# An exchange through DRAM: all four of its writes issued by SyncE instead of two by SyncE and two by ScalarE

## The chip, the cores and the metric

The kernel runs on one core of a Trainium2 chip. The metric is the device time of one execution in microseconds (us), median over runs. The engines are named as the profile names them: PE (TensorE matmul), PEld (its weight loads), DVE (VectorE), ACT (ScalarE), POOL (GpSimd) and SP (SyncE). A "q" behind a name (SPq, ACTq) is the engine's sequencer, which issues DMAs.

## The reference

For x of 8 sequences x 128 tokens x 512 features, all in float32, the reference computes two residual blocks:

```python
x = x + ffn0(lora_matmul(x, weight[ids]))      # 8 adapters; top-2 of 8 low-rank experts
x = x + ffn1(attention(x))                     # below; then top-16 of 64 rank-8 experts

q = rope(rmsnorm(x @ Wq)); k = rope(rmsnorm(x @ Wk)); v = x @ Wv   # 32 q heads, 8 kv heads, D = 128
k_all = concat(k_cache[pages], k); v_all = concat(v_cache[pages], v)   # 512 cached + 128 new keys
p = softmax(mask(q @ k_all.T * D**-0.5)); y = (p @ v_all) @ Wo
```

Four query heads share one kv head. The cached keys and values lie in pages of 32 tokens, found through a table of page numbers; keys beyond a sequence's length are masked.

## The kernel before, in words

The first block runs in a stage of its own (about the first 120 us). The attention then runs as 64 *units*. A unit is one sequence and one kv head with its 4 query heads; two units in a row are the two kv heads of one *step* and share the step's cached keys and values. The order of all instructions is written out by hand, with no scheduler: each engine executes its own in program order, and semaphores between engines follow from the data.

`iteration(u)` is the pipeline. In it PE computes the scores of unit u, head by head (`scores`, L793 and L796), then the output projection of unit u-3 (`output`, L895), a slice of the q, k, v projection of a later unit (`project`, L259), and last the product of probabilities and values of unit u-2 (`values`, L873). DVE adds the mask and scales (`mask_exp`, L806), ACT takes the exponential (L817), DVE the reciprocal of its sum (L822), POOL scales by it (L823).

The probabilities have to be turned (keys on the partitions) before PE can use them. PE doesn't do that. DVE transposes blocks of 32 x 32 within groups of 32 partitions (`blocks`, L828, and `blocks_qk`, L779, for the rotated q and k of unit u+2) into the tile pb. What is left is to move whole blocks between the four groups of 32 partitions, and that is done by DMA through DRAM:

- `exchange_out(u)` (L840) writes pb to a DRAM tile px with four DMAs, one for each group of 32 partitions (i = 0 to 3). Each moves 32 x 4 rows of 3200 bytes (2560 where no later q and k ride along).
- `exchange_in(u)` (L850 and L853, both SP), one iteration later, reads qkb (q and k of unit u+2) and pT (the probabilities) back from px, block-transposed.

pb has one buffer, so L779 of the next unit can't write into it until all four writes have read it. px has three DRAM buffers, qkb one, pT two. From qkb ACT makes qkT, the queries and keys for the scores (`heads_qk`, L860), between the last exponential and the sums of squares of a later unit (`norms`, L308). POOL turns those into rs (L314), and DVE needs rs to rotate k (L340) right after the exchange. ACT also copies the attention output o to oT (`evict_o`, L884) at the head of the next iteration.

SP has, in program order, in each iteration: three pages of cached keys (`gather`, L193 to L194: for each page it loads a page number into a register, then issues a DMA of 32 KB), `exchange_in(u-1)`, the other pages (seven in even units, three in odd ones), in some iterations a load of ya (L143) and a store to yd (L919) of a partial sum, and at the end its part of `exchange_out(u)`. POOL issues the weights (L153, L177) and gathers the values vt (L204) from its own queue. ACT issues no DMA in the attention except its part of the exchange. In the DMA view queue q1 is SP's, q10 ACT's, q0 POOL's.

Of the kernel before, what the change touches and what calls it, by code (L numbers as in the profile page):

```python
# [33 lines left out]
QD = P // 32  # L34
# [23 lines left out]
def adaln_ffn_kernel(  # L58
# [25 lines left out]
    nc = tc.nc  # L84
# [667 lines left out]
    with ExitStack() as l1:  # L752
# [80 lines left out]
        def exchange_out(u):  # L833

            pb = pb_t.pop(u)
            m = dram_x.tile([QD, 32, QD, XW], F32, tag="px", name=f"px_{u}")
            w = XW if u + 2 in range(3, NU) else PW
            for i in range(QD):
                eng = nc.sync if i < QD // 2 else nc.scalar
                eng.dma_start(  # L840
                    out=m[:, :, i, :w].rearrange("k b f -> b k f"),
                    in_=pb[i * 32 : (i + 1) * 32, :, :w],
                )
            px_t[u] = m
# [114 lines left out]
        def iteration(u):  # L959
# [98 lines left out]
            if on(u):  # L1058
                blocks(u, REP - 2)
                blocks(u, REP - 1)  # L1060
                exchange_out(u)
# [176 lines left out]
```

## Time and profile before

| | before |
|---|---|
| median of 3 runs | 1248.08 us |
| lowest, highest | 1246.36, 1251.02 us |
| the profiled execution, its own time | 1243.45 us |
| its span (first to last instruction) | 1241.7 us |
| granted TensorE clock | 0.997 |
| mean DMA rate over the span | 241 GB/s |

The page describes the one profiled execution. Its span is 1.75 us shorter than its time. "Busy" is the time in which an engine executed instructions of the program. A timeline line gives the start, the length (of the merged run of instructions), the engine and line, what is written from what, how many instructions, and in brackets how long the engine had stood idle and what ended it. A line of the stages view gives, for a stretch of the span, each engine's busy time and number of instructions, the granted clock, the busy share of the 16 DMA engines and what they moved. The trace also holds a record of each DMA packet: its queue, size, start and length.

### The profile page before, as it was taken

To read this page: it belongs to the slowest core of one execution; us is meant where nothing else is said; L and a number is where in the kernel's file an instruction comes from. 1 tells how busy PE (TensorE), PEld (TensorE's weight loads), DVE (VectorE), ACT (ScalarE), POOL (GpSimd) and SP (SyncE) were. 2 spreads that over 40 slices of the span, in tenths; PEclk is the share of its full clock that TensorE was granted. 3 is DMA by queue.
4 is the path that set the end of the run, shared out by engine and by line. 5 is a ranking of instruction groups with operands and counts; after the bars stand their busy time and mean duration, and the time that the engine had idled before them with its cause. 6 is when DMAs were issued, how large, how long until landed. Compare 5 with 4: busy or idle time off the path is not lost.

```text
span 1241.7 us, 15991 instructions
## 1 busy us (share of the span) xinstructions
PE 1224.1 (99%) x3847; PEld 650.6 (52%) x3847; DVE 902.4 (73%) x2045; ACT 506.6 (41%) x1457; POOL 590.7 (48%) x687
## 2 busy tenths in 40 slices
PE   8999899999999999999999999999999999999998
PEld 7765455554555555555455555554555555555444
DVE  2546798889877777788877777788777777787522
ACT  1334444444444444444444444444444444443211
POOL 2443565575544555555445545655445544553100
PEclk9999999999999999999999999999999999999999
DMA  8822777788878877888878778888878777787512
GB/s 303 304 79 94 223 233 249 234 274 286 271 234 257 259 244 249 284 277 281 266 258 268 252 243 260 287 284 275 257 242 281 248 235 231 259 269 269 178 51 85
DMA packets 204785, 298.99 MB, mean 241 GB/s; under 512 B 84563, under 2 KB 116564, under 8 KB 203796
## 3 DMA queue, kind: packets, MB, share of 16 engines
q1 hardware_dynamic: 173092, 205.41, 52.6%
q10 hardware_dynamic: 18720, 52.49, 12.0%
q0 software_dynamic: 12880, 40.08, 9.4%
q8 instruction: 31, 0.51, 0.2%
q14 instruction: 62, 0.51, 0.1%
HBM read 183.54 MB, written 114.36 MB: 240 GB/s over the span
## 4 chain that ended last, share of the span: by engine, by line
PE 88%; DVE 4%; DMA 3%; ACT 2%; issue 1%; POOL 1%; ACTq 1%; SPq 0%; DVEq 0%; POOLq 0%
PE o L873 19%; PE p L259 18%; PE y L895 16%; PE s L793 16%; PE s L796 4%; PE p L292 2%; PE bp L517 2%; PE op L1130 2%; PE cp L495 2%; PE fz L701 2%; DMA px<-pb 1%; DVE wqkv L163 1%; ACT sq L308 1%; DMA kt<-in_kc 1%; DVE p L806 1%
## 5 line engine op out<-in xcount | busy, mean ns | idle before, releaser
L823 POOL TENSOR_SCALAR p<-p,den 128x640 f32<-128x640 f32 x256 | 211.8, 827 | 424.0 <-DVE den L822 423.4
L817 ACT ACTIVATE p<-p,low 128x640 f32<-128x640 f32 x256 | 212.0, 828 | 437.3 <-DVE den L822 297.4
L806 DVE CUSTOM_DVE_ANT_0 p<-s,mask,rs 128x640 f32<-128x640 f32 x256 | 224.0, 879 | 109.1 <-PE s L796 106.0
L259 PE MATMUL p<-wqkv,xo 128*128 128x384 f32 x784 | 280.4, 486 | 0.0
L895 PE MATMUL y<-wo,oT 128*128 128x512 f32 x512 | 262.5, 597 | 5.4 <-ACT oT L884 5.4
L793 PE MATMUL s<-kt,qkT 128*128 128x512 f32 x504 | 258.6, 595 | 3.2 <-ACT qkT L860 2.7
L873 PE MATMUL o<-pT,vt 128*128 128x512 f32 x512 | 230.2, 592 | 0.0
L259 PEld LDWEIGHTS p<-wqkv,xo 128*128 128x128 f32 x784 | 148.9, 190 | 139.8 <-issue 73.1
L828 DVE STREAM_TRANSPOSE pb<-p 128x640 f32<-128x640 f32 x252 | 207.7, 824 | 16.9 <-POOL p L823 16.9
L796 PEld LDWEIGHTS s<-qkT 128*128 128x128 f32 x504 | 96.2, 191 | 121.1 <-issue 121.1
L873 PEld LDWEIGHTS o<-pT,vt 128*128 128x128 f32 x512 | 97.3, 190 | 110.3 <-issue 95.2
L204 POOL DMA_INDIRECT vt<-in_vc,vrow x128 | 135.9, 1062 | 39.3 <-issue 27.7
L793 PEld LDWEIGHTS s<-kt,qkT 128*128 128x128 f32 x504 | 95.5, 191 | 98.2 <-issue 55.0
L314 POOL TENSOR_TENSOR rs<-ss,mhalf 128x5 f32<-128x5 f32 x64 | 99.7, 1558 | 5.3
L308 ACT ACTIVATE sq<-c 128x128 f32<-128x128 f32 x320 | 98.8, 309 | 8.1
L796 PE MATMUL s<-qkT 128*128 128x128 f32 x504 | 97.2, 275 | 0.0
L884 ACT COPY oT<-o 128x512 f32<-128x512 f32 x64 | 37.5, 586 | 144.8 <-PE o L873 139.4
L895 PEld LDWEIGHTS y<-wo,oT 128*128 128x128 f32 x512 | 78.6, 192 | 11.4 <-ACT oT L884 6.8
L262 DVE TENSOR_TENSOR c<-c,p 128x384 f32<-128x384 f32 x84 | 45.3, 539 | 31.2 <-PE p L259 31.2
L873 PE MATMUL o<-pT,vn 128*128 128x512 f32 x128 | 65.4, 592 | 0.0
L308 ACT ACTIVATION_READ_ACCUMULATOR sq<-c 128x1 f32 x320 | 59.7, 186 | 0.0
L779 DVE STREAM_TRANSPOSE pb<-ca 128x640 f32<-128x640 f32 x61 | 50.5, 828 | 6.8 <-DMA px<-pb 5.9
(181 smaller groups left out, 1178.9 us busy)
## 6 DMA issues: line engine op xcount, KB each, us to landing
pT<-px SPq DMA_DIRECT2D x64, 1280.0 KB, 6.6
px<-pb SPq DMA_DIRECT2D x122, 400.0 KB, 5.5
px<-pb ACTq DMA_DIRECT2D x122, 400.0 KB, 6.4
qkb<-px SPq DMA_DIRECT2D x61, 320.0 KB, 3.4
kt<-in_kc SPq DMA_DIRECT2D x512, 32.0 KB, 4.6
wqkv<-in_wqkv POOLq DMA_DIRECT2D x32, 384.0 KB, 5.1
yd<-ya SPq DMA_DIRECT2D x24, 256.0 KB, 3.1
wo<-in_wo POOLq DMA_DIRECT2D x12, 512.0 KB, 4.5
```

Of the source, the lines that this page charges most:

```text
L204: nc.gpsimd.indirect_dma_start(out=kv_t[step][1][:, c, :], out_offset=None, in_=vc, in_offset=bass.IndirectOffsetOnAxis(ap=vrow[:, hf, at ...
L259: nc.tensor.matmul(out=ps, lhsT=xo[:, pr, x, c, :], rhs=w[:, c, :], start=(c == 0), stop=(c == 1))
L308: nc.scalar.activation(sq, cs[:, at : at + D], AF.Square, accum_out=ss[:, h : h + 1])
L314: nc.gpsimd.tensor_tensor(rs, ss, mhalf, ALU.pow)
L793: nc.tensor.matmul(out=s[:, :L], lhsT=qkT[:, h, :], rhs=kt[:, :, g % GH, :], start=True, stop=True)
L796: nc.tensor.matmul(out=s[:, L:NK], lhsT=qkT[:, h, :], rhs=qkT[:, REP, :], start=True, stop=True)
L806: nc.vector.tensor_tensor_reduce(out=p, in0=s_t.pop((u, h))[:, :NK], in1=mask_t[st], scale=rs_t[u][:, h : h + 1], scalar=BIG, op0=ALU.add, ...
L817: nc.scalar.activation(p, p, AF.Exp, bias=low, scale=-1.0, accum_out=den)
L823: nc.gpsimd.tensor_scalar(p_t[u, h], p_t[u, h], den, 1.0, ALU.mult, ALU.mult)
L828: nc.vector.transpose(pb_t[u][:, :, h * w : (h + 1) * w].rearrange("p i (j a) -> p j i a", a=32), p_t.pop((u, h)).rearrange("p (j i a) -> ...
L873: nc.tensor.matmul(out=o, lhsT=vt[:, c, j * D : (j + 1) * D] if c < LC else vn_t.pop(u), rhs=pT[:, c], start=(c == 0), stop=(c == LC),)
L895: nc.tensor.matmul(out=y_t[st], lhsT=oT_t[u][:, h, :], rhs=wo_t[g][:, h, :], start=(h == 0 and j == 0), stop=(h == REP - 1 and j == GH - 1),)
```

## The change

Before, the writes of i = 0 and 1 (partitions 0 to 63) are issued by SP and those of i = 2 and 3 (partitions 64 to 127) by ACT. After, SP issues all four, one after another, and ACT none. Nothing else differs: the data, the tiles, their buffers and the order of all other instructions are the same.

```diff
             for i in range(QD):
-                eng = nc.sync if i < QD // 2 else nc.scalar
-                eng.dma_start(
+                nc.sync.dma_start(
                     out=m[:, :, i, :w].rearrange("k b f -> b k f"),
                     in_=pb[i * 32 : (i + 1) * 32, :, :w],
                 )
```

## The prediction

> **What bounds the kernel now.** I read the busy table first, then the DMA queues, then SyncE's and VectorE's timelines over one exchange.
>
> ```profile
> PE 1224.1 (99%) x3847; PEld 650.6 (52%) x3847; DVE 902.4 (73%) x2045; ACT 506.6 (41%) x1457; POOL 590.7 (48%) x687
> ...
> q1 hardware_dynamic: 173092, 205.41, 52.6%
> q10 hardware_dynamic: 18720, 52.49, 12.0%
> ```
>
> PE is never free: whatever costs nothing on PE costs nothing. ScalarE at 41% gains little from fewer issues. q10 is ScalarE's queue: it carries the px writes of partitions 64 to 127 (2 a unit) and little else. q1 is SyncE's: the other two px writes, qkb, pT, pages, y. The waits show only 8.6 us in which PE stood idle in the attention stage, nearly all behind ScalarE (2.7 for qkT, 5.4 for oT; the longest at 150.6, 154.5 and 856.4 us). So a gain is small, and a loss must first use up the slack.
>
> The stages view, two stretches inside exchanges: in the first only ScalarE's two writes are moving, in the second all four.
>
> ```profile
> core 0: us, PE busy (x) PEld busy (x) DVE busy (x) ACT busy (x) POOL busy (x), PEclk, DMA share, GB/s
> 153.50:156.50 3.00, 2.02 (x3) 0.99 (x4) 1.69 (x3) 0.59 (x1) 2.80 (x4) 0.50 0.97 207
> ...
> 623.00:625.00 2.00, 2.00 (x7) 0.98 (x6) 1.71 (x5) 0.37 (x1) 1.68 (x3) 1.00 1.03 395
> ```
>
> The DMA engines are full in both (0.97 and 1.03), yet half the partitions alone move 207 GB/s and both halves together 395. The packet records agree: a 3200-byte packet takes about 245 ns in the first, 126 to 136 ns in the second. SyncE's timeline from one exchange (odd unit 17) to the next:
>
> ```profile
> 403.53 0.85 SPq L840 DMA_DIRECT2D px<-pb  x2
> 405.48 3.52 SPq L194 DMA_DIRECT2D kt<-in_kc  x3
> 411.86 0.54 SPq L850 DMA_DIRECT2D qkb<-px  x1
> 412.45 0.62 SPq L853 DMA_DIRECT2D pT<-px  x1
> 413.58 5.38 SPq L194 DMA_DIRECT2D kt<-in_kc  x7
> 419.02 0.42 SPq L143 DMA_DIRECT2D ya<-yd  x1
> 419.54 0.38 SPq L919 DMA_DIRECT2D yd<-ya  x1
> 420.87 0.32 SPq L840 DMA_DIRECT2D px<-pb  x1
> ```
>
> From write to qkb, L = 8.33 us here (median 7.7), SyncE waits for the writes to land. Then it needs 8.06 us (411.86 to 419.92) before it can issue the next exchange, which came 17.34 us after the last: about 1 us to spare. VectorE in the unit before:
>
> ```profile
> 396.13 0.83 DVE L779 STREAM_TRANSPOSE pb<-ca 128x640 f32<-128x640 f32 x1
> ...
> 398.48 0.88 DVE L806 CUSTOM_DVE_ANT_0 p<-s,mask,rs 128x640 f32<-128x640 f32 x1 [0.35 <-PE s L796]
> ...
> 400.63 0.56 DVE L262 TENSOR_TENSOR u<-u,p 128x384 f32<-128x384 f32 x1 [0.44 <-PE p L259]
> ```
>
> L779 is the first to refill pb, of which there is one buffer, so it needs the four writes finished. It starts 8.40 us after the exchange at 387.73 (9.82 in even units). The exchange follows 7.39 us later, of which 0.35 + 0.44 + 0.2 us is waiting that lateness can use.
>
> [...]
>
> **The change part by part.**
> 1. *Issue.* 128 writes leave ScalarE (122 of 400 KB, 6 of 320 KB), at a median 0.37 us: 47 us of its sequencer, nearly all beside idle time. What shows on PE is the wait of 1.61 us at 856.4 (ScalarE held by issues of 2.88 us) and some 1.0 of 2.3 us at 154.5: **-2**, bounds 0 and -4. SyncE issues two more, 0.85 us a unit, while it would otherwise wait for the landing: 0. The three page loads behind move by 0.85 us and still end before the landing. DVE and POOL issue nothing new.
> 2. *Transfer.* Now one ring holds partitions 0-31, 32-63, 64-95, 96-127 in this order. [...] The four writes are 1.638 MB: at 207 GB/s 7.9 us, at 395 4.15. Unit 2 of this trace already ran its halves one after the other: 153.07 to 160.99 us, 7.92. From issue to first packet 0.83 us, from last packet to the qkb issue 0.45: **L = 9.2 us** in a quiet unit, against 7.7. Bounds: 7.7 (engines drift apart and use both halves) and 9.5 (the 4096-byte value gathers are not hidden in it).
> 3. *Who waits.* DVE L779, and behind it the transposes of p, the adds that free PE's kv bank (room before PE stalls: 2.3 us), the softmax and the exchange itself. SyncE L850, and behind it pT, seven pages, y and the next exchange. ScalarE's qkT copy: 9.2 + 3.4 = 12.6 us, needed at 12.56 or 14.01: just met; PE needs it 5 us later.
> 4. *Quiet units.* Odd: L779 is late by 9.2 - 8.4 = 0.8 us, and 0.99 absorbs it. Even: 9.2 + 8.06 = 17.3 of 17.35. Cost 0. But the loop of exchange, landing, exchange now has no slack: for two units 2L + 8.06 + 6.44 against 33.13 us gives a limit of **L = 9.3**; above it every 0.1 us is paid.
> 5. *Loaded units.* Where weights and y stand ahead in the queues, SyncE's first px packet (packet records) comes later than 0.83 us: 2.11, 2.46, 3.95 (units 24, 26, 28), 3.59, 2.49, 2.34, 2.58 (38, 40, 42, 44). ScalarE's half did not stand behind q1's share. With 7.9 + 0.45 the seven L are 10.5, 10.8, 12.3, 11.9, 10.8, 10.7, 10.9; over 9.3 together 12.8 us. Their odd neighbours (1.14 to 1.35 before the first packet) add some 1.2. PE can let VectorE fall 2.3 us behind once in each of the two stretches: -4.6. **+9.4**.
> 6. *Start-up.* PE waits for qkT at 150.6 already; unit 1's L grows from 8.72 to 1.09 + 7.9 + 0.45 = 9.44: **+0.7**.
>
> Sum: -2 + 9.4 + 0.7 = **+8 us** on the profiled execution's 1243.45 (span 1241.70 and 1.75 around it). That execution lies 4.6 us under the median of the three, so I add the 8 to the median: 1256.
>
> **The rivals.**
> *Hidden.* The DMA engines drift apart, so L stays under 8.8, and the lateness is absorbed everywhere: PE's 99% and the waits of SyncE (up to 1.5 us ahead of even exchanges, over 3 us ahead of odd ones) speak for it, the 7.92 us of unit 2 against. Time: 1248 - 2 to + 4, so 1246 to 1252, not slower. It decides if issue to qkb is at most 8.8 us in quiet units.
> *ScalarE relieved.* Only its waits count: all of -4 and L unchanged, 1244. To be over 0.5% faster it would need 6.2 us, more than the 5.4 us that PE ever waited for oT; nearly excluded.
> *Loop everywhere.* L is 9.5 in quiet units too; the some 22 pairs of quiet units at 2 x 0.2 = 0.4 us add 9 to the 8, and lateness from a loaded unit is never made up before the next, which costs the 4.6 of step 5 and more: +17 to +30, so 1265 to 1278. [...]
> The change does move the writes: the order of SyncE's instructions shows four px writes in a row, ScalarE's none.
>
> **How the numbers follow.** Forecast (+4 to +16): 0.44; loop everywhere 0.23; hidden 0.29; relieved, and what no step foresees, 0.04. Half a per cent, 6.2 us, is about what a measurement of this kernel can tell from no change. Of the forecast's case a fifth lies under that. Slower by over 0.5%: 0.44 x 0.8 + 0.23 = 0.58; within: 0.29 + 0.09 = 0.38; faster: 0.04. The range runs from 1245 (hidden, with ScalarE's relief) to 1278 (loop everywhere); the forecast's own is 1252 to 1264.
>
> **What would show it.** Right: q10 nearly empty; about 207 GB/s for most of an exchange; the qkb issue 9 us or more after the first px write; VectorE's L779 waiting on px far over 5.9 us in total; SyncE's wait for pb at L840 well under 146 us; PE idle near 570 to 620 and 755 to 870 us. Wrong: 300 GB/s or more in an exchange with one ring, or a landing as late as forecast with PE still at 99%; then steps 2 or 4 and 5 fail.

## The result, and the profile after

| | before | after |
|---|---|---|
| median | 1247.79 us (5 runs) | 1292.5 us (5 runs) |
| lowest, highest | 1244.65, 1251.02 us | 1291.23, 1296.65 us |
| ratio after / before | | 1.0371, 95% interval 1.0353 to 1.0388 |
| the profiled execution, its own time | 1243.45 us | 1296.65 us |
| its span | 1241.7 us | 1294.9 us |
| granted TensorE clock | 0.997 | 0.989 |

The change costs 44.7 us by the medians. The two profiled spans differ by 53.2 us, because the profiled execution of before lies under its median and that of after is the slowest of its five. The working below explains the 53.2.

The page of after: busy times, the two hardware queues, and the chain that ended last. The line under it is the chain of before.

```profile
PE 1245.3 (96%) x3847; PEld 650.5 (50%) x3847; DVE 899.0 (69%) x2045; ACT 503.6 (39%) x1457; POOL 597.2 (46%) x687
...
q1 hardware_dynamic: 191524, 257.36, 68.5%
...
q10 hardware_dynamic: 288, 0.54, 0.1%
...
PE 52%; DMA 22%; SPq 10%; issue 6%; DVE 5%; POOL 2%; ACT 1%; DVEq 0%; POOLq 0%; ACTq 0%
```

```profile
PE 88%; DVE 4%; DMA 3%; ACT 2%; issue 1%; POOL 1%; ACTq 1%; SPq 0%; DVEq 0%; POOLq 0%
```

q1 carries 52 MB more and q10 nothing worth naming: the writes did move. The bytes are the same, yet the two queues' share of the DMA engines' time rose from 64.6% to 68.6%: a px packet of 3200 bytes takes 202 ns on the mean, 159 before. The chain ran along PE for 88% of the span and does so for 52%; DMA and SP's sequencer now hold almost a third of it. PE is idle for 49.6 us, 32 more than before, and busy for 21.2 us more with the same 3847 matmuls, which no step of the prediction foresaw.

SP's timeline of after, from one odd exchange (unit 21) to the next:

```profile
483.87 4.28 SPq L839 DMA_DIRECT2D px<-pb  x4
489.19 3.83 SPq L194 DMA_DIRECT2D kt<-in_kc  x3
493.42 0.54 SPq L849 DMA_DIRECT2D qkb<-px  x1
494.01 0.62 SPq L852 DMA_DIRECT2D pT<-px  x1
495.14 5.38 SPq L194 DMA_DIRECT2D kt<-in_kc  x7
500.83 0.33 SPq L143 DMA_DIRECT2D ya<-yd  x1
501.25 0.38 SPq L918 DMA_DIRECT2D yd<-ya  x1
501.72 4.71 SPq L839 DMA_DIRECT2D px<-pb  x4
```

(From L839 on, after's line numbers are one lower than before's.) L, from the first write to the qkb issue, is 9.55 us here. Three things differ from before. The four writes hold SP for 4.28 and 4.71 us, where two held it for 0.85. The three pages behind them end at 493.02, only 0.4 us before the qkb issue (2.9 us in before's exchange, in the prediction). And the next exchange follows 0.09 us after the store to yd: SP is never ahead any more. In the even units 5 to 56 SP has less than 0.2 us to spare in 23 of 26; before, in 3.

The same exchange in the stages view. Its packets run from 484.70 to 492.84 us:

```profile
core 0: us, PE busy (x) PEld busy (x) DVE busy (x) ACT busy (x) POOL busy (x), PEclk, DMA share, GB/s
485.00:488.00 3.00, 2.44 (x8) 1.13 (x8) 1.59 (x6) 0.59 (x1) 2.42 (x4) 1.00 0.95 196
489.00:492.00 3.00, 3.00 (x10) 1.56 (x10) 1.81 (x6) 1.85 (x4) 0.80 (x1) 1.00 0.99 289
```

For the first two writes, the DMA engines are full (0.95) and move 196 GB/s: half the 395 of before with both halves in flight. In the second stretch other transfers run beside the writes (59 of the 289 GB/s are from POOL's queue). The exchange as a whole moves 1.638 MB in 8.14 us, or 201 GB/s.

And the waits that this makes, first DVE's and PE's, then SP's:

```profile
DVE pb L779 <- DMA px<-pb: 70.1, 35, 4.4
...
PE p L259 <- DVE c L262: 25.0, 18, 4.2
```

```profile
SPq L839 <- DVE pb L828: 85.0, 32, 5.2
...
SPq L849 <- DMA px<-pb: 19.9, 39, 3.8
```

The same waits of DVE and SP in before:

```profile
DVE pb L779 <- DMA px<-pb: 5.9, 6, 2.7
```

```profile
SPq L840 <- DVE pb L828: 146.2, 56, 6.5
```

L779 waited for px for 5.9 us in before, 70.1 now; in the odd units 5 to 56 it waits over 0.2 us in all 26 (7 before). PE then waits at L259, for a bank that VectorE empties late (L262). SP's wait for pb fell from 146.2 to 85.0 us: that was its slack.

### The profile page after: what moved, and what is told of

The parts are those of the page before. It is cut to its first block, busy times and chain, and to the rows that moved or that the text cites. A ratio compares the mean times of both kernels' runs of the same rounds, so it can differ in the third digit from the quotient of the medians.

```text
span 1294.9 us, 15928 instructions
## 1 busy us (share of the span) xinstructions
PE 1245.3 (96%) x3847; PEld 650.5 (50%) x3847; DVE 899.0 (69%) x2045; ACT 503.6 (39%) x1457; POOL 597.2 (46%) x687
## 4 chain that ended last, share of the span: by engine, by line
PE 52%; DMA 22%; SPq 10%; issue 6%; DVE 5%; POOL 2%; ACT 1%; DVEq 0%; POOLq 0%; ACTq 0%
DMA px<-pb 14%; PE o L872 10%; PE p L259 9%; PE s L793 9%; PE y L894 9%; DMA pT<-px 5%; SPq L839 5%; DMA kt<-in_kc 2%; DVE pb L828 2%; PE s L796 2%; PE p L292 2%; PE bp L517 2%; PE op L1129 2%; PE cp L495 2%; SPq L194 2%
## 5 line engine op out<-in xcount | busy, mean ns | idle before, releaser
L259 PE MATMUL p<-wqkv,xo 128*128 128x384 f32 x784 | 290.9, 496 | 25.0 <-DVE c L262 25.0
L793 PE MATMUL s<-kt,qkT 128*128 128x512 f32 x504 | 262.3, 602 | 11.6 <-DMA px<-pb 4.3
L806 DVE CUSTOM_DVE_ANT_0 p<-s,mask,rs 128x640 f32<-128x640 f32 x256 | 221.0, 876 | 71.7 <-PE s L796 70.6
L259 PEld LDWEIGHTS p<-wqkv,xo 128*128 128x128 f32 x784 | 148.6, 192 | 173.5 <-issue 77.4
L872 PE MATMUL o<-pT,vt 128*128 128x512 f32 x512 | 233.5, 599 | 0.0
L828 DVE STREAM_TRANSPOSE pb<-p 128x640 f32<-128x640 f32 x252 | 207.3, 823 | 19.6 <-POOL p L823 19.6
L779 DVE STREAM_TRANSPOSE pb<-ca 128x640 f32<-128x640 f32 x61 | 51.2, 839 | 92.5 <-DMA px<-pb 70.1
L314 POOL TENSOR_TENSOR rs<-ss,mhalf 128x5 f32<-128x5 f32 x64 | 85.0, 1328 | 5.3
L312 POOL TENSOR_SCALAR ss<-ss,eps 128x5 f32<-128x5 f32 x64 | 48.1, 751 | 73.0 <-ACT sq L308 73.0
L340 DVE SCALAR_TENSOR_TENSOR ca<-c,rs,tab 128x128 f32<-128x128 f32 x64 | 24.8, 387 | 65.2 <-POOL rs L314 65.2
```

What stands on the lines that cost most here:

```text
L259: nc.tensor.matmul(out=ps, lhsT=xo[:, pr, x, c, :], rhs=w[:, c, :], start=(c == 0), stop=(c == 1))
L314: nc.gpsimd.tensor_tensor(rs, ss, mhalf, ALU.pow)
L793: nc.tensor.matmul(out=s[:, :L], lhsT=qkT[:, h, :], rhs=kt[:, :, g % GH, :], start=True, stop=True)
L806: nc.vector.tensor_tensor_reduce(out=p, in0=s_t.pop((u, h))[:, :NK], in1=mask_t[st], scale=rs_t[u][:, h : h + 1], scalar=BIG, op0=ALU.add, ...
L828: nc.vector.transpose(pb_t[u][:, :, h * w : (h + 1) * w].rearrange("p i (j a) -> p j i a", a=32), p_t.pop((u, h)).rearrange("p (j i a) -> ...
L872: nc.tensor.matmul(out=o, lhsT=vt[:, c, j * D : (j + 1) * D] if c < LC else vn_t.pop(u), rhs=pT[:, c], start=(c == 0), stop=(c == LC),)
```

## The experiments

**Theories.** *Halves* (theory A of the expectations): the loss comes from writes that are all of one half of the partitions at a time (207 GB/s in before, against 395 with both halves moving), which the order within one ring brings about; a ring is one issuer's DMA queue, q1 or q10. *Issuer* (theory B): it comes from SP issuing and queueing all of it, whichever partitions come first. L is read in each trace as the time from the first px write's issue to the qkb issue, W as the time from the first px packet to the last; single values are medians over the exchanges 1 to 61 (before: L 7.8, W 6.3). The kernel before lay between 1245.5 and 1246.6 us beside these runs. "Pair" is the mean time of two units, over the 26 pairs of units 5 to 56.

### Two issuers, the same or different halves at a time

e1_in_phase: SP issues 0 and 2, ACT 1 and 3, so that both start with partitions 0 to 63.

```diff
-                nc.sync.dma_start(
+                eng = nc.sync if i % 2 == 0 else nc.scalar
+                eng.dma_start(
```

> Two issuers as before, but SP issues the groups i = 0 and 2, ACT i = 1 and 3, so both queues hold first a write of partitions 0 to 63 and then one of 64 to 127. Theory A [...]: the px packets of a unit take 7.5 to 8.2 us from first to last as in the changed kernel (8.06 there, 6.27 before), the qkb issue comes 9.0 to 9.5 us after the first write, and the time is 1265 to 1290 us. Theory B (one queue: [...] stands behind SP's other transfers, and SP is busy 4.3 us with issuing): two queues are back, so 6.3 us, 7.8 us and 1245 to 1252 us.

e2_anti_phase: the same, but SP issues 0 then 2 and ACT 3 then 1.

```diff
-            for i in range(QD):
+            for i in (0, 3, 2, 1):
+                eng = nc.sync if i % 2 == 0 else nc.scalar    # then eng.dma_start, as in e1
```

> Two issuers, SP issues i = 0 then 2, ACT i = 3 then 1: at any time the two queues are in different halves. Theory A and theory B both expect the time of the kernel before, 1243 to 1252 us, and packets of a unit within 6.0 to 6.5 us. Against the run with both queues in the same half it shows what the order of the halves alone does, with the same number of issues on each engine: A expects 20 to 40 us between the two, B none.

Measured: e1 1286.09 us, 1.0331 (1.0304 to 1.0357), median L 9.82 and W 8.35 us. e2 1253.46 us, 1.0055 (1.0035 to 1.0075), just over what was expected, L 8.08, W 6.66. The two differ in nothing but which ACT write comes first. The stages view inside an exchange, four writes in two rings, of e1 and then of e2:

```profile
451.00:454.00 3.00, 3.00 (x11) 1.57 (x10) 1.72 (x5) 0.59 (x1) 2.48 (x3) 1.00 0.96 201
```

```profile
441.40:442.40 1.00, 1.00 (x4) 0.50 (x3) 0.93 (x3) 0.00 (x0) 0.53 (x1) 1.00 1.02 394
```

e1 moves the same 201 GB/s as the exchange with one ring, e2 twice that. e2's rate doesn't last: two us later in the same exchange it is 278 GB/s. Its L after even exchanges is 9.05 us against 8.27 in before, so it isn't quite the kernel before.

With ACT's help back in full and only the halves in step, some 40 of the 45 us stay lost; the order of two instructions is worth 33 us, where *issuer* expected none. The issuer alone is not the cause. The lateness reaches PE by another way in e1, though. PE hardly waits at L259 (2.9 us), but for oT, which ACT copies:

```profile
PE y L895 <- ACT oT L884: 20.7, 17, 3.6
```

That was 5.4 us in before and 3.7 in after. So e1 shows that the halves cost the time, and not that the time is lost on the same path as in after.

### One ring, whole height

e3_one_write: SP issues the exchange as one DMA of all 128 partitions. e9_four_full: SP issues four DMAs of 400 KB, as in after, but each covers all partitions and a quarter of the columns. Both leave out the order of the blocks in DRAM that the reads rely on, so they time the transfer and don't compute the reference.

```diff
-                    out=m[:, :, i, :w].rearrange("k b f -> b k f"),
-                    in_=pb[i * 32 : (i + 1) * 32, :, :w],
+                nc.sync.dma_start(out=mp[i, :, :w], in_=pb[:, i, :w])   # e9 (cut); mp = m as [k, 128, f]
```

> SP alone issues the exchange, as one write of all 128 partitions with the same bytes (the blocks land in DRAM in another order than the reads expect, so the attention uses wrongly ordered probabilities; sizes, reads and all other work are the same). [...] Theory A: the packets of a unit take 4.2 to 5.5 us, the qkb issue comes 5.7 to 7 us after the write, and the time is 1240 to 1249 us. Theory B (one queue is the cost): the packets are still in one ring behind SP's other transfers, about 8 us, and 1280 to 1293 us.

> SP alone issues four writes of 400 KB each, as in the changed kernel, but each holds all 128 partitions and one quarter of their columns (the blocks land in DRAM in another order than the reads expect, so the probabilities are wrongly ordered; sizes, reads and all other work are the same). Number of DMAs, bytes, rows of 3200 bytes and the ring are those of the changed kernel; only the partitions of each differ. Theory A [...]: as with the one write, packets of a unit within 4.5 to 5.5 us, the qkb issue 5.9 to 6.8 us after the first write, 1235 to 1241 us. Rival (four issues one after another on SP, its sequencer held 4.3 us a unit): 1270 to 1293 us.

Measured: e3 1235.91 us, 0.9922 (0.9903 to 0.9941), faster than expected, L 5.87, W 4.56. e9 1235.58 us, 0.9916 (0.9895 to 0.9936), L 6.74, W 4.68. e9's stages view inside an exchange, then SP's timeline, then SP's waits:

```profile
399.60:403.20 3.60, 3.60 (x12) 1.69 (x11) 2.95 (x7) 0.59 (x1) 2.79 (x3) 1.00 1.00 385
```

```profile
398.68 2.40 SPq L840 DMA_DIRECT2D px<-pb  x4
```

```profile
SPq L840 <- DVE pb L828: 192.5, 59, 6.9
```

Number, size, ring and issuer are those of after, yet the kernel is 57 us faster than after (1292.5 - 1235.6) and 11 faster than before. The rows also lie in other places in DRAM; but in before they lie as in after, and there a packet takes 126 to 136 ns when both halves are in flight. The places are not what makes packets slow. 385 GB/s take the place of 196; even SP's issue takes 2.40 us instead of 4.28. SP waits for pb for 192.5 us, so it has slack again.

Three things follow. One ring cost nothing here when each of its DMAs spanned both halves (e9, 385 GB/s); for writes of part of the height, a second issuer in the other half was worth 45 us (before), one in the same half some 4 (e1). The rates went with the halves that were moving, not with the rings: 201 GB/s from two rings in step (e1), 385 from one ring of the full height; what in the hardware makes it so isn't shown. And the kernel before is slower than e9: of 7.8 us between the profiled spans, 4.5 lie in the 26 pairs (33.30 against 33.12 us) and 3.1 ahead of them. How much of this is its L of 7.8 and how much ScalarE's issues, which e9 doesn't have, the runs don't separate. Between e3's 5.9 and e9's 6.7 us there is no gain left.

### SP's backlog: the pages

In even units SP issues seven late pages and y, in odd ones three. e5_pages_even makes it five and five on top of after; e7_before_pages does the same to before.

```diff
-            first, end = ((0, 10), (10, NPP))[u % GH]
+            first, end = ((0, 8), (8, NPP))[u % GH]
```

> The changed kernel, with the 16 key pages of a step split 8 and 8 over its two units instead of 10 and 6. The landing of the writes stays as late as in the changed kernel (qkb issue 9.4 to 9.9 us after the first write). Theory A with the loop (exchange, landing, SP's page loads, next exchange sets the pace at 2L + 8.06 + 6.44 us for two units): the even unit loses 1.7 us of SP's work and is then set by VectorE's part, 2L + 12.9 = 32.4 us at L = 9.75, under PE's 33.13; the time falls to 1250 to 1268 us. Rival (the late landing itself, or lost issue time, costs the 45 us, whatever SP does after it): 1285 to 1293 us as changed.

> The kernel before (two issuers), with the key pages split 8 and 8. With L at 7.8 us SP has the even unit's 1.7 us to spare, and lateness in loaded units is made up faster; the last pages of the odd unit land about 18 us after the exchange, just before the next scores. Expected: within 4 us of the kernel before, 1241 to 1249 us; if pages land too late, PE waits for kt and it is 1250 to 1258.

Measured: e5 1274.89 us, 1.0232 (1.0215 to 1.0249), above what was expected; the pair went from 35.08 to 34.28 us. e7 1246.97, 0.9994 (0.9975 to 1.0012). So in after SP's work in even units is a limit, worth some 18 us, and in before it was none. That e5 didn't gain more has two reasons. L779 still waits over 0.2 us in 23 of the 26 odd units, 1.06 us on the mean (2.71 in after). And PE has a wait that was 0.8 us in after:

```profile
PE s L793 <- DMA kt<-in_kc: 15.2, 10, 2.9
```

Pages that come later in the odd units are late for the scores.

### SP's backlog: y

e6_y_by_pool lets POOL issue the y load and store (`nc.gpsimd` for `nc.sync` at L143 and L918); e10_y_by_act lets ACT issue them, late in the unit.

```diff
-                nc.sync.dma_start(out=y_d[st % B], in_=ya_t.pop(st))
+                nc.gpsimd.dma_start(out=y_d[st % B], in_=ya_t.pop(st))    # e6
+                store_t.append(st)     # e10: issued by nc.scalar after the sums of squares; the load likewise (cut)
```

> The changed kernel, with the loads of ya and the stores to yd issued by POOL instead of SP (0.4 to 0.9 us less for SP in every second unit, and none of their 256 KB ahead of the px writes in SP's ring). Loop theory: SP's time from the qkb issue to the next exchange falls from 8.66 to about 7.5 us and the write after the even unit starts with less in front of it (L 9.7 instead of 10.07), so a pair of units takes 35.1 - 1.1 - 0.4 = 33.6 us, and the time falls by 25 to 40 us to 1252 to 1268. Rival (VectorE's wait for pb alone sets the pace, SP is only late because of it): no more than 8 us better, 1284 to 1293 us.

> The changed kernel, with the loads of ya and the stores to yd issued by ACT, after the squares and the copy of v, where ACT's px writes stood before. Neither SP nor POOL has them. If SP's lateness before every even exchange holds part of the pace: SP's time from the qkb issue to its next exchange falls from 8.66 to about 7.1 us, the even unit from 18.4 to 17.5 us, and 26 pairs give 20 to 26 us back: 1266 to 1274. Rival (VectorE's wait for pb sets the pace in both units): 1285 to 1293 us.

Measured: e6 1292.94 us, 1.0372 (1.035 to 1.0395), a miss: its rival had the range. SP needs 1.25 us less in even units and is 1.21 us ahead there, and still the pair stays at 35.07. Waits of DVE, then of POOL, in e6:

```profile
DVE pb L779 <- DMA px<-pb: 91.3, 43, 4.5
...
DVE pb L828 <- POOL p L823: 49.7, 63, 2.5
```

```profile
POOL yd L918 <- DVE den L822: 31.6, 24, 1.7
```

The second line was 19.6 us in after: POOL's y DMAs stand ahead of its scaling of p and hold it up (third line), so VectorE is late by about what SP gained. e10 avoids that: 1281.81, 1.0297 (1.0255 to 1.0339), between the two expectations. Even units fell from 18.42 to 17.52 us as meant, odd ones rose by 0.2. SP has no more slack there than in after (0.19 us on the mean). SP's backlog and VectorE's wait for pb both hold the loop; lightening one uncovers the other.

### How much L may be: spare writes

e11_two_more and e12_four_more add two and four writes of 400 KB to e9, to a DRAM tile that is never read. Like e9 they leave out the order of the blocks.

```diff
+                x = dram_x.tile([QD, P, XW], F32, tag="spare", name=f"spare_{u}")
+                for i in range(2):                                        # 4 in e12
+                    nc.sync.dma_start(out=x[i], in_=pb[:, i, :])
```

> Four full-height writes from SP (wrongly ordered blocks as in that run) and behind them two more of 400 KB each, of the same pb into a spare DRAM tile that nobody reads; pb is free when all six have read it. [...] each write takes some 1.05 us at 395 GB/s, so packets take 6.7 us and pb is free some 8 us after the first issue, while qkb is issued at 6 to 6.5 us, or 8 if the later packets share the engines. Loop theory: under the limit of 9.3 us, so the time stays within 1235 to 1248 us. Rival (each us of exchange time costs in proportion, some 10 us of time for each us as from 6 to 7.8 us between the four full writes and the kernel before): 1250 to 1258.

> As the run with two more writes, with four more: packets take some 8.8 us, and pb is free only some 10 us after the first issue; qkb and pT need only the first four writes. The DMA engines work about as long as in the changed kernel (512 packets of 200 ns or 1024 of 130). Loop theory: VectorE's part of the loop is over its limit, so 1265 to 1295 us with VectorE waiting long for px at L779; SP's part is not late through landing, but its reads and pages stand behind the four extra writes in the ring. Rival (only the half-height writes are costly, by whatever means): 1240 to 1255 us.

Measured: e11 1276.53 us, 1.0238 (1.0202 to 1.0275), L 9.1, W with the spares 7.63; e12 1396.62 us, 1.1202 (1.1163 to 1.1242), L 11.2, W 9.77. Both missed, on the slow side. A wait of DVE in e11, and the longest of PE in e12:

```profile
DVE pb L779 <- DMA spare<-pb: 43.2, 21, 4.9
```

```profile
PE p L259 <- DVE c L262: 83.5, 27, 4.8
```

At L779 VectorE waits 2.2 us in the mean odd unit of e11 and 5.0 in e12, where e9 has 0.01. With full-height packets (about 131 ns on the mean, 202 in after) a long landing is costly too, so the time of the exchange counts, and not only its half-height packets. The spare writes also add 50 and 100 MB of traffic; that this costs something beside the longer landing isn't excluded. L and pace, means over units 5 to 56:

| | L after odd + after even exchange, us | pair, us |
|---|---|---|
| e9 | 6.73 + 7.12 = 13.85 | 33.12 |
| before | 7.79 + 8.27 = 16.06 | 33.30 |
| e2 | 8.03 + 9.05 = 17.08 | 33.79 |
| e11 | 8.86 + 9.42 = 18.28 | 34.46 |
| after | 9.58 + 10.07 = 19.65 | 35.08 |
| e1 | 9.94 + 10.11 = 20.05 | 34.70 |
| e12 | 11.02 + 11.62 = 22.64 | 38.47 |

From e11 to e12 the pair grows by 4.01 us for 4.36 us of L: nearly all of it is paid, as in a loop without slack. Followed back at that rate, the pair leaves 33.12 at a sum of 16.8, or 8.4 us an exchange. For half-height writes that is a lower estimate, because after and e1 lie 0.6 and 1.4 us under this line. With after's own other terms (below) the limit comes out at (33.30 - 8.84 - 6.58) / 2 = 8.9. Before lies under both, e2 near the first, the others over them.

### Whole-height writes with the data in their places

With whole-height writes the four groups of 32 partitions must be told apart in the reads. e8_split_reads: one write, and qkb and pT read as four DMAs each, of 32 partitions, all by SP, in the order 0, 2, 1, 3. e13_shared_reads: groups 0 and 1 by SP, 2 and 3 by ACT.

```diff
-                nc.sync.dma_start(out=qkb, in_=m[:, :, PW:])
+                for k in (0, 2, 1, 3):                                     # e8; pT likewise, write as in e3 (cut)
+                    nc.sync.dma_start(out=qkb[k * 32 : (k + 1) * 32],
+                        in_=m[k, :, PW:XW].rearrange("(i b) f -> b i f", b=32))
```

> All of the exchange on SP, with the regrouping moved to the reads: one write of 128 partitions, and qkb and pT each read by four DMAs of 32 partitions (in the order 0, 2, 1, 3). The landing of the write falls to 4.6 us as in the one-write run; SP issues six more DMAs for the reads (2 to 3 us a unit), [...] pT 6.3 us instead of 3.3, but it has an iteration to spare. [...] the qkb read, alone at the head, costs about 1 us more, the time is 1236 to 1252 us. If SP's extra issues or the DMA engines' time decide (busy 78% before), 1252 to 1290.

> A version that may beat both: SP issues the exchange as one write of 128 partitions (in an order that the reads undo), and qkb and pT are each read by four DMAs of 32 partitions, SP those of partitions 0 to 63, ACT those of 64 to 127, after ACT's second exponential of the next unit, some 6 us after the write, when it has landed. The half-height transfers are now reads on two rings in different halves. [...] write landed after 4.6 to 5.9 us, reads as fast as before, 1235 to 1246 us. If ACT's issues (four a unit, some 1.7 us) come in the way of its exponentials, or ACT's reads start later than SP's: 1246 to 1275 us.

Measured: e8 1275.3 us, 1.024 (1.0208 to 1.0273), L 6.87. e13 1263.55, 1.0139 (1.0088 to 1.0191), L 6.6. PE's waits, e8 then e13:

```profile
PE s L793 <- DMA kt<-in_kc: 20.7, 8, 5.2
```

```profile
PE s L793 <- DMA kt<-in_kc: 12.4, 7, 3.6
```

The landing is quick, but now the reads are the transfers of part of the height. They stand ahead of the pages in SP's ring, and SP also needs longer: from the qkb issue to its last issue of an even unit 11.0 us in e8 and 10.8 in e13, against 8.3 in before. PE waits for keys. Which of the two makes the pages late isn't separated. Two issuers cut the loss from 29 to 17 us. Neither comes near e9, and neither beats the kernel before.

## Why the prediction was right and wrong

The direction and the course of the loss were right: about half the rate in an exchange (201 GB/s over the one shown, where 207 were forecast), SP's slack gone, L779 waiting. The size was not: +8 us forecast, +45 measured, beyond the range. The nearest rival, "loop everywhere", had the better picture, since every exchange of after has an L over 9.2 us, but with +17 to +30 was too small too.

**Step 1, issue.** The extra issues were costed at nothing beside SP's wait. The four took 4.3 to 4.8 us rather than 2 x 0.85, so the pages behind end 0.4 us before the qkb issue instead of 2.9. In the exchange shown that is still hidden; the cover is nearly used up. ScalarE's relief was put at 2 us; PE's waits for oT fell from 5.4 to 3.7 us, so 1.7. (The 47 us of its sequencer is the median times 128; the issues add up to 59.7 us, which changes nothing here.)

**Step 2, transfer.** The packets were sized right: 7.9 us forecast, 8.06 measured (median W). The first packet was not: 0.83 us after odd exchanges as forecast, but some 1.6 after even ones, because SP issues those right behind its own seven pages, ya and yd, which lie ahead in the same ring. In before, where SP had more slack, it was 1.2; in e6, where POOL issues ya and yd, it is 0.84. L is 9.58 after odd and 10.07 after even exchanges, against 9.2 for both.

**Step 4, quiet units: the step that failed.** It costed them at 0, with a limit of L = 9.3. They cost 1.78 us a pair. The loop's form was right; the terms were small. By the means over the 26 pairs:

| term | forecast | measured in after |
|---|---|---|
| L after odd exchange | 9.2 | 9.58 |
| SP from qkb to the next exchange, even unit | 8.06 | 8.66 + 0.18 waiting |
| L after even exchange | 9.2 | 10.07 |
| VectorE from L779 to the exchange, odd unit | 6.44 | 6.58 |
| a pair | 32.9, under 33.13 | 35.08 |

8.06 was read off one exchange; the mean of before was 8.33. Each term is out by 0.1 to 0.9 us, 2.2 together; the slack was 0.2. Against before's 33.30 the pair lost 1.78 us, and 26 of them make 46.4 of the 53.2 us; the start adds 2.0 and the end 4.8. Where the time of an odd unit is lost is seen in VectorE's timeline, at the unit after the exchange at 467.57:

```profile
477.47 0.84 DVE L779 STREAM_TRANSPOSE pb<-ca 128x640 f32<-128x640 f32 x1 [2.08 <-DMA px<-pb]
```

It starts 9.90 us after the exchange and has waited 2.08 us of that. The forecast had 0.8 us, absorbed by later waits.

The limit was also taken as sharp. The experiments point to a gradual one, at 8.4 to 8.9 on the mean: e2, with a median L of 8.1, is already 18 us slower than e9, 17 of them in the pairs. A sign of it was there in before: 7 of before's 26 odd units already waited at L779.

**Step 5, loaded units.** It gave PE's cushion once per stretch and let the lateness end with the stretch. It took those units for the place of the loss, with L of 11.1 us on the mean of the seven. They have 10.3 in after, and all even exchanges 10.1: no unit is quiet, nothing is made up, and of PE's long stalls (1.9 us or more) those near 413, 547, 725 and 941 us lie outside the stretches that were named. The step's +9.4 has no counterpart that can be told apart in the trace. **Step 6, start-up**: +0.7 forecast, +2.0 measured up to unit 4.

**Not in any step: the clock.** Both kernels have a stretch of half the granted clock near 151 us, 6.83 us long. After has six more in the attention, of 3.41 us each. The stages view of after in one of them, and PE's timeline ahead of another:

```profile
622.10:625.40 3.30, 3.30 (x6) 1.58 (x6) 3.19 (x8) 2.48 (x9) 2.43 (x3) 0.50 1.03 373
```

```profile
870.97 2.68 PE L259 MATMUL p<-wqkv,xo 128*128 128x384 f32 x4 [4.21 <-DVE c L262]
```

In the first, PE runs without a gap, but six matmuls fill 3.30 us; in the second, four take 2.68 us that take 1.29 at the full clock. Each of the six begins near the end of a stall of PE, 1.9 to 4.2 us long (from 0.5 us before the end to 1.4 us after it). In e9 PE has no stall over 1.5 us in the attention, and no such stretch there (mean granted clock 1.0). Six halves of 3.41 us are 10 us, about half of the 21 us by which PE's busy time grew; the other half isn't accounted for. A late VectorE thus cost PE more than the wait here. How much of the 10 us lies inside the loop's lateness, and so isn't added to it, the runs don't tell.

**What stays open.** How the loss divides between SP's backlog and VectorE's wait for pb: e5, e6 and e10 each moved one and met the other. A second pb buffer, which would take VectorE's wait away alone, wasn't tried.

## What to carry to other kernels

Look at which partitions of a transfer are moving at once, and not only at its queues and bytes. Here DMAs of 32 partitions, two of one half after two of the other in one ring, moved about 200 GB/s; DMAs of the full height, or two rings on different halves, moved 385 to 395. Before an edit that lengthens a transfer in a loop of "write, land, refill", take each term of the loop as a mean over many rounds, once for odd and once for even, and treat any slack of less than the terms' spread as spent. When an issuer loses its slack, its own earlier transfers can come to lie ahead of the urgent one: here the first packet after even exchanges came 1.6 us after the issue, where before had 1.2 and e6, with ya and yd on POOL, 0.84.

## What the runs showed of the hardware

- SP's issue of four DMAs of 400 KB isn't of fixed cost: 4.3 to 4.8 us when they move some 200 GB/s (after), 2.4 us when they move 385 (e9).
- The stretches of half the granted clock were 3.41 us long (six in after) or twice that, 6.83 us (near 151 us, in before and after). In after, all six came with a stall of PE. The length of the stall alone doesn't decide: in after one of 1.88 us (at 547.09) was enough, in e1 one of 2.76 us (at 886.92) was not. In e12 such stretches add up to 107 us and bring the mean clock to 0.962.
